# Two-layer transformer block: the second attention is queued by clocks of the engines, which also choose VectorE or GpSimd for each addition of the bias

## The chip, the cores and the metric

The kernel runs on one core of a Trainium2 chip. The metric is the time of one execution on the device in microseconds (us); smaller is better. A core has five engines, each with a queue of its own that it works off in order: TensorE (PE, products; its weight loads are listed as PEld), VectorE (DVE), ScalarE (ACT), GpSimd (POOL) and SyncE (SP), which here only issues transfers (DMA). Engines wait for each other by semaphores.

## The reference

Input `x` is 8 x 512 x 256 in fp32. Layer 0 adds a causal attention (with a latent of 64 for keys and values) and a gated feed-forward of ternary weights to `x`; layer 1 adds an attention with a bias of position and a routed mixture of small experts. What the change orders anew is the attention of layer 1:

```python
qkv = jnp.einsum('bsd,ed->bse', xn, Wqkv)
q, k, v = jnp.split(qkv, 3, axis=-1)            # 16 heads of 16
logits = jnp.einsum('bihd,bjhd->bhij', q, k) * scale + pos_bias[None]
attn = jax.nn.softmax(logits, axis=-1)
out = jnp.einsum('bhij,bjhd->bihd', attn, v).reshape(B, S, D)
x = x + jnp.einsum('bsd,ed->bse', out, Wout) + experts(xn)
```

The bias depends on head and distance alone.

## The kernel before

Four stages follow each other: the first attention, the feed-forward, the second attention, the experts. Between them `x` goes through DRAM (`x1d`, `x2d`, `x3d`; the normalised `x` of layer 1 through `xn1d`, its transposed form through `xt1d`), one image of 512 tokens at a time, in tiles of 128 partitions.

Both attentions are objects of the class `Attention`. An image has 4 jobs of 4 heads each. For one job the queries and keys are loaded from DRAM as high and low fp32r parts, stacked over the partitions (`load`, four transfers on SyncE's queue, with one of four stacks). Then come

- 16 units of `first` (L280): a product `s_ps` of 128 queries with 512 keys for one head, and on VectorE one instruction that adds the bias and takes the smallest value of each row (the signs are turned, so this is the maximum). `ps_s` has three banks.
- `maxima` (L303): the 16 columns of row values are split in two parts, transposed, copied by ScalarE and sent into two more rows of the stack of queries by two transfers, so that the next product subtracts them by itself.
- 16 units of `second` (L324): the product `t_ps` of 128 keys with 512 queries. In the second attention the bias is then added in one of two ways: by VectorE out of PSUM (L348), or by a copy on ScalarE (L350) and an addition on GpSimd in SBUF (L351). `ps_t` has two banks. `exp` (L373) takes the exponential of two heads at once, in place.
- 4 `weigh` (L378): four products of the weights with the values, one per head, summed over the key tiles in one bank `ctx_ps`.
- `take` and `finish`: ScalarE copies the result, TensorE transposes it, VectorE divides by the sums; after the fourth job the output projection is added to `x`.

The order of all instructions is written out by `run` (L455) under a manual schedule: all five queues follow the program's order. A step `n` has four slots. Each slot queues one `first` (six steps ahead, `lag`), one `second`, in slots 0 and 2 an `exp` of the step before, in slot 0 a `weigh` of two steps before, then one piece of the closing work (`close`) and one piece of the work that prepares the next image (`tasks`: `prep_here`, `values1`). `pause` puts two empty pieces between pieces that depend on each other. Which engine adds the bias is fixed:

```python
if r == 0 or (r == 1 and n % 2):
    nc.vector.tensor_tensor(pt[:, r, :], ps, bias, ALU.add)
else:
    nc.scalar.copy(pt[:, r, :], ps)
    nc.gpsimd.tensor_tensor(pt[:, r, :], pt[:, r, :], bias, ALU.add)
```

So of the 64 additions of an image 24 are VectorE's and 40 are GpSimd's. Closing and preparing work of the second attention share the two banks of `ps_m`. `prep_here(b)` normalises, transposes and projects an image and sends queries and keys to DRAM; `values1(b)` makes its values.

In the experts, `go_down` (L1081) makes the products `d_ps`, copies them to `down` (three buffers) and stores them to DRAM (`inter`); for every 16 experts' pairs four gathers bring them back by token group (`back`), and `combine` adds them to `x` and stores `out`. All these transfers are issued on SyncE's queue, where an issue that waits holds up the ones behind it.

Of the kernel before, what the change touches and what calls it, by code (L numbers as in the profile page):

```python
# [21 lines left out]
P = 128  # L22
# [40 lines left out]
def block_kernel(ctx: ExitStack, tc: tile.TileContext, a: dict, out: bass.AP):  # L63
# [15 lines left out]

    x = {}  # L80

    def fetch_x(pool, b, src, tag="x", to=x):
        to[b] = pool.tile([P, TPB, D], F32, tag=tag, name="x")
        nc.sync.dma_start(to[b], src[b * S : (b + 1) * S, :].rearrange("(t p) d -> p t d", p=P))

    def leave_x(b, dst):
        nc.sync.dma_start(dst[b * S : (b + 1) * S, :].rearrange("(t p) d -> p t d", p=P), x[b])

    x1d = dram.tile([B * S, D], F32, name="x1d")
    x2d = dram.tile([B * S, D], F32, name="x2d")  # L90
    x3d = dram.tile([B * S, D], F32, name="x3d")
    xnd = dram.tile([B * P, 2 * S], F32, name="xnd")
    xn1d = dram.tile([B * S, D], F32, name="xn1d")
# [17 lines left out]
    nc.gpsimd.memset(power, -0.5)  # L111
# [5 lines left out]
    def norm_steps(layer, b, pool):  # L117
        for t in range(TPB):
            st = pool.tile([P, 6], F32, tag="bn", name="bn")
            nc.vector.bn_stats(st, x[b][:, t, :])  # L120
            nc.vector.bn_aggr(mv[:, layer, b * TPB + t, :], st)
            if t % 2:
                yield
        ve = pool.tile([P, TPB], F32, tag="ve", name="ve")
        nc.vector.tensor_scalar_add(ve, mv[:, layer, b * TPB : (b + 1) * TPB, 1], EPS)  # L125
        yield
        r0 = pool.tile([P, TPB], F32, tag="r0", name="r0")
        nc.gpsimd.tensor_tensor(r0, ve, power, ALU.pow)  # L128
# [3 lines left out]
        nc.vector.tensor_mul(r2, r0, r0)  # L132
        nc.vector.tensor_mul(r2, r2, ve)
        nc.vector.tensor_scalar(r2, r2, -0.5, 1.5, ALU.mult, ALU.add)
        nc.vector.tensor_mul(rstd[:, layer, b * TPB : (b + 1) * TPB], r0, r2)

    def normalise(layer, b, t, dst, src=None):
        i = b * TPB + t
        nc.vector.tensor_scalar(
# [8 lines left out]
    def transpose_steps(srcs, dst, psum, tag, evacuate):  # L148
        for i in range(0, len(srcs), 2):
            ps = psum.tile([P, 2, 2, P], F32, tag=tag, name="xT_ps")  # L150
            for j in range(2):
                for d in range(2):
                    nc.tensor.transpose(ps[:, d, j, :], srcs[i + j][:, d * P : (d + 1) * P], ident)
# [14 lines left out]
    def split(pool, ps, scale, dst, reverse, bufs):  # L168
# [4 lines left out]
        nc.scalar.activation(hi[:, way], ps, AF.Copy, scale=scale)  # L173
# [3 lines left out]
        nc.vector.scalar_tensor_tensor(lo[:, way], ps, scale, hi[:, way].bitcast(F32), ALU.mult, ALU.subtract)  # L177
# [16 lines left out]

    def pause():

        for _ in range(2):
            yield

    class Attention:  # L200
# [4 lines left out]
        def __init__(self, st, causal, order, lag, stacks, qd, kd, bias_of, w_out, fetch, done, cn_bufs):  # L205
# [10 lines left out]
            self.ps_m = pool("ps_m", 2, space=PSUM)  # L216
# [14 lines left out]
            self.jobs = {}  # L231
            if causal:
                self.mask = self.fixed.tile([P, S], F32, name="mask")
                nc.scalar.dma_start(self.mask, a["cst"][:, C_CAUSAL:])
# [7 lines left out]
        def clear(self, i):  # L242

            qs, ks = self.stacks[i]
            nc.gpsimd.memset(qs[64:, :, :].bitcast(F32), 0.0)
            nc.gpsimd.memset(ks[64:, :, :].bitcast(F32), 0.0)
            nc.gpsimd.memset(ks[ROW_M : ROW_M + 2, :, :].bitcast(F32), -1.0)
            if i < len(self.vst):
                nc.gpsimd.memset(self.vst[i], 1.0)


        def keep_v(self, b, t, v_ps, copy=nc.vector.tensor_copy):

            assert b < len(self.vst) or (b - len(self.vst), 3) in self.taken
# [25 lines left out]
        def first(self, s, r):  # L280
# [6 lines left out]
            nc.tensor.matmul(  # L287
# [11 lines left out]
            nc.vector.tensor_tensor_reduce(  # L299
# [3 lines left out]
        def maxima(self, t):  # L303
# [4 lines left out]
            nc.vector.tensor_copy(by_tile[0], job["least"])  # L308
            nc.vector.tensor_tensor(by_tile[1], job["least"], by_tile[0].bitcast(F32), ALU.subtract)
# [4 lines left out]
            nc.tensor.transpose(ps, parts.rearrange("p l r c -> p (l r c)").bitcast(F32), ident)  # L314
            yield True
            rows = self.work.tile([2 * n, P], F32R, tag="rows", name="rows")
            nc.scalar.copy(rows, ps)
            for part in range(2):
                (nc.scalar if self.causal else nc.sync).dma_start(
                    job["qs"][ROW_M + part : ROW_M + part + 1].bitcast(F32), rows[part * n : (part + 1) * n, :].bitcast(F32)  # L320
                )
            yield

        def second(self, n, r):  # L324
# [3 lines left out]
            lo = j * P if self.causal else 0  # L328
# [9 lines left out]
            nc.tensor.matmul(  # L338
# [6 lines left out]
            if not self.causal:  # L345
                bias = self.bias_of(self.order[t][1], r, j)
                if r == 0 or (r == 1 and n % 2):
# [867 lines left out]
```

## Time and profile before

| | us |
|---|---|
| median of 3 runs | 2205.24 |
| lowest and highest run | 2197.03, 2216.65 |
| the profiled execution | 2195.91 |
| its span, first to last instruction | 2194.2 |

The stages of the profiled execution, by windows of its trace:

| stage | from, to | length | PE busy | DVE busy | ACT busy | POOL busy | DMA share |
|---|---|---|---|---|---|---|---|
| first attention | 0 to 575 | 575 | 479.81 | 380.33 | 241.26 | 121.97 | 0.61 |
| feed-forward | 575 to 1250 | 675 | 660.40 | 323.29 | 155.62 | 8.02 | 0.12 |
| second attention, loads | 1250 to 1296 | 46 | 23.73 | 23.91 | 3.04 | 21.68 | 0.88 |
| second attention | 1296 to 1930 | 634 | 586.75 | 510.14 | 471.16 | 412.93 | 0.46 |
| its end | 1930 to 1945 | 15 | 5.03 | 2.06 | 0.58 | 2.82 | 0.35 |
| experts | 1945 to 2194 | 249 | 174.78 | 98.13 | 67.10 | 42.74 | 0.84 |

In the profile, a group's line gives line of code, engine, operation, output<-inputs, shapes and count, then busy time and the mean of one in ns, then the idle time of the engine just before these instructions and the instructions that ended most of it. A matmul's busy time includes waiting inside the pipeline; the spacing of starts tells what one costs.

### The profile page before, as it was taken

To read this page: it belongs to the slowest core of one execution; us is meant where nothing else is said; L and a number is where in the kernel's file an instruction comes from. 1 tells how busy PE (TensorE), PEld (TensorE's weight loads), DVE (VectorE), ACT (ScalarE), POOL (GpSimd) and SP (SyncE) were. 2 spreads that over 40 slices of the span, in tenths; PEclk is the share of its full clock that TensorE was granted. 3 is DMA by queue.
4 is the path that set the end of the run, shared out by engine and by line. 5 is a ranking of instruction groups with operands and counts; after the bars stand their busy time and mean duration, and the time that the engine had idled before them with its cause. 6 is when DMAs were issued, how large, how long until landed. Compare 5 with 4: busy or idle time off the path is not lost.

```text
span 2194.2 us, 29805 instructions
## 1 busy us (share of the span) xinstructions
PE 1930.5 (88%) x10182; PEld 1259.3 (57%) x10182; DVE 1337.9 (61%) x3621; ACT 938.8 (43%) x1570; POOL 610.1 (28%) x552
## 2 busy tenths in 40 slices
PE   3689999999799999999999779999999999968863
PEld 1345555555488888888888544544544444436652
DVE  3667776677345535535535367888878878735431
ACT  0244444445322212212222137777777778834320
POOL 4211111112100000000000256656656657732200
PEclk8799999999899999999999879999999999989986
DMA  5647767674430000000001384554553554167697
GB/s 126 177 121 175 185 164 195 174 173 109 181 127 30 20 10 29 20 1 20 20 1 49 90 238 98 117 124 91 116 127 89 114 121 77 47 235 204 192 254 204
DMA packets 151905, 254.40 MB, mean 116 GB/s; under 512 B 14382, under 2 KB 84911, under 8 KB 151395
## 3 DMA queue, kind: packets, MB, share of 16 engines
q1 hardware_dynamic: 146418, 245.56, 43.2%
q10 hardware_dynamic: 4864, 6.24, 0.9%
q8 instruction: 82, 1.34, 0.3%
q0 software_dynamic: 464, 0.63, 0.1%
q14 instruction: 77, 0.62, 0.1%
HBM read 171.58 MB, written 91.29 MB: 120 GB/s over the span
## 4 chain that ended last, share of the span: by engine, by line
PE 62%; DMA 12%; DVE 10%; ACT 4%; issue 4%; POOL 1%; SPq 1%; ACTq 1%; POOLq 0%; DVEq 0%
PE hid_ps L780 21%; PE t_ps L338 7%; PE ctx_ps L385 7%; PE s_ps L287 6%; PE proj_ps L522 3%; DMA qs<-rows 3%; DVE junk L299 3%; DMA ks<-kd 3%; PE val L780 3%; PE gate L780 3%; PE ffo L780 2%; PE o_ps L443 2%; DMA back<-inter 1%; DMA inter<-down 1%; PE d_ps L1092 1%
## 5 line engine op out<-in xcount | busy, mean ns | idle before, releaser
L287 PE MATMUL s_ps<-ks,qs 96*128 96x512 f32 (+2 forms) x1024 | 471.0, 468 | 81.6 <-DMA ks<-kd 40.4
L351 POOL TENSOR_TENSOR pt<-pt,bias 128x512 f32<-128x512 f32 x320 | 408.8, 1288 | 242.5 <-ACT pt L350 233.5
L338 PE MATMUL t_ps<-qs,ks 128*128 128x512 f32 (+2 forms) x1024 | 394.8, 391 | 38.1 <-DMA qs<-rows 15.1
L299 DVE CUSTOM_DVE_ANT_0 junk<-s_ps,bias 128x512 f32<-128x512 f32 x512 | 338.0, 686 | 120.3 <-PE s_ps L287 107.2
L287 PEld LDWEIGHTS s_ps<-ks,qs 96*128 96x128 f32 x1024 | 201.9, 198 | 265.6 <-DVE least L299 110.7
L299 DVE CUSTOM_DVE_ANT_0 junk<-s_ps,mask 128x384 f32<-128x384 f32 (+3 forms) x512 | 233.1, 486 | 142.0 <-PE s_ps L287 140.8
L338 PEld LDWEIGHTS t_ps<-qs,ks 128*128 128x128 f32 x1024 | 197.9, 195 | 149.1 <-ACT pt L350 43.2
L376 ACT ACTIVATE pt<-pt 128x1024 f32<-128x1024 f32 x256 | 273.7, 1069 | 3.2 <-POOL pt L351 3.1
L770 DVE CAST h<-hf 128x512 fp32r<-128x512 f32 x192 | 81.2, 426 | 303.2 <-ACT hf L819 302.2
L385 PE MATMUL ctx_ps<-pt,vst 128*32 128x512 f32 (+3 forms) x2048 | 262.5, 533 | 3.7 <-ACT pt L376 2.5
L819 ACT ACTIVATE hf<-hid_ps,sh 128x512 f32<-128x512 f32 x128 | 88.1, 688 | 380.5 <-PE hid_ps L780 374.6
L350 ACT COPY pt<-t_ps 128x512 f32<-128x512 f32 x320 | 184.3, 585 | 151.8 <-PE t_ps L338 150.3
L780 PE MATMUL hid_ps<-h,h1T_m 128*128 128x512 f32 x1024 | 237.4, 391 | 0.0
L780 PE MATMUL hid_ps<-h,h2T_m 128*128 128x512 f32 x1024 | 236.9, 392 | 0.0
L780 PEld LDWEIGHTS hid_ps<-h,h2T_m 128*128 128x128 f32 x1024 | 192.2, 188 | 42.6 <-issue 2.9
L780 PEld LDWEIGHTS hid_ps<-h,h1T_m 128*128 128x128 f32 x1024 | 191.2, 188 | 43.8 <-DVE h L771 2.5
L128 POOL TENSOR_TENSOR r<-ve,power 128x4 f32<-128x4 f32 x16 | 16.2, 1012 | 706.9 <-DVE ve L125 602.9
L363 POOL TENSOR_SCALAR_AFFINE_SELECT pt<-pt 128x512 f32<-128x512 f32 x128 | 81.7, 639 | 404.6 <-ACT pt L353 229.6
L353 ACT ACTIVATE pt<-t_ps 128x512 f32<-128x512 f32 (+1 forms) x256 | 130.3, 546 | 99.9 <-PE t_ps L338 95.0
L348 DVE TENSOR_TENSOR pt<-t_ps,bias 128x512 f32<-128x512 f32 x192 | 131.6, 685 | 15.4 <-PE t_ps L338 14.0
L771 DVE TENSOR_TENSOR h<-hf,h 128x512 fp32r<-128x512 f32 x192 | 132.0, 690 | 5.6
L355 ACT ACTIVATE pt<-t_ps 128x256 f32<-128x256 f32 (+1 forms) x128 | 61.9, 491 | 148.3 <-PE t_ps L338 117.1
(137 smaller groups left out, 2265.2 us busy)
## 6 DMA issues: line engine op xcount, KB each, us to landing
qs<-qd SPq DMA_DIRECT2D x128, 256.0 KB
ks<-kd SPq DMA_DIRECT2D x64, 256.0 KB
ks<-kd SPq DMA_DIRECT2D x128, 128.0 KB
inter<-down SPq DMA_DIRECT2D x32, 512.0 KB
back<-inter SPq DMA_DIRECT2D x32, 512.0 KB
qd<-hi SPq DMA_DIRECT2D x32, 256.0 KB
qd<-lo SPq DMA_DIRECT2D x32, 256.0 KB
kd<-hi SPq DMA_DIRECT2D x32, 256.0 KB
```

Of the source, the lines that this page charges most:

```text
L287: nc.tensor.matmul(ps[:, :n], lhsT=job["qs"][:ROW_M, r, c * P : (c + 1) * P], rhs=job["ks"][:ROW_M, r, :n], start=True, stop=True,)
L299: nc.vector.tensor_tensor_reduce(junk[:, :width], ps[:, :width], add, 1.0, 3e38, ALU.add, ALU.min, job["least"][:, c, r : r + 1])
L338: nc.tensor.matmul(ps[:, base - at : S - at], lhsT=job["ks"][:, r, j * P : (j + 1) * P], rhs=job["qs"][:, r, base:], start=True, stop=True,)
L348: nc.vector.tensor_tensor(pt[:, r, :], ps, bias, ALU.add)
L350: nc.scalar.copy(pt[:, r, :], ps)
L351: nc.gpsimd.tensor_tensor(pt[:, r, :], pt[:, r, :], bias, ALU.add)
L353: nc.scalar.activation(pt[:, r, lo:], ps[:, lo:], AF.Exp, scale=-1.0)
L376: nc.scalar.activation(pt, pt, AF.Exp, scale=-1.0)
L385: nc.tensor.matmul(job["ctx"][32 * r : 32 * r + 32, lo:], lhsT=job["v"][:, j, r, :], rhs=job["p"][j][:, r, lo:], start=(j == 0), stop=(j = ...
L771: nc.vector.tensor_tensor(t[1][:, k, :], value, t[0][:, k, :].bitcast(F32), ALU.subtract)
L780: nc.tensor.matmul(ps, lhsT=l, rhs=r, start=(i == 0), stop=(i == len(pairs) - 1))
L819: nc.scalar.activation(hf, ps, AF.Gelu, scale=scales[sc][:, o : o + 1])
```

## The change

The method `run_by_clock` takes the place of `run` for the second attention. While it writes the program it keeps a clock for each of PE, DVE, ACT and POOL. Every instruction is issued through a small wrapper (`T_`, `V_`, `A_`, `G_`) that moves its engine's clock on by an assumed duration; the instruction itself is the same. 0.6 us are assumed for a hand-over from one engine to another. At each turn the method looks at what could start on TensorE at its present clock (a first product, a second product, a weighing, a piece of closing work, a piece of preparing work), each with the time at which its inputs and its bank would be there, and queues the first that qualifies in a fixed order of preference. If nothing qualifies, TensorE's clock moves on.

```diff
+    HANDOVER = 0.6
+    def takes(engine, op, out, k):
+        if engine == "PE":
+            if op == "transpose":
+                return 0.15
+            n = columns_of(k["rhs"]) * (1 if k["rhs"].dtype == F32R else 4)
+            return 0.013 + n / 2400 * (0.25 if k["lhsT"].shape[-1] == 2 * HD else 1)
+        n = columns_of(out)
+        if engine == "DVE":
+            return 0.08 + n / 960
+        if engine == "ACT":
+            return 0.45 if op == "dma_start" else 0.12 + n / 1140
+        return 0.1 if op == "dma_start" else 0.2 + n / (470 if op == "tensor_tensor" else 4700 / 4)
```

The second products of this attention have their own method, in which the clocks choose the engine of the addition:

```diff
+        def second_biased(self, n, r, at, exps):
...
+            bias = self.bias_of(self.order[t][1], r, j)
+            by_pool = max(clock["POOL"], max(clock["ACT"], at) + 0.5 + HANDOVER) + 1.3
+            if max(clock["DVE"], at) + 0.6 < by_pool - 3.0:
+                V_.after = at
+                V_.tensor_tensor(pt[:, r, :], ps, bias, ALU.add)
+                free = added = clock["DVE"]
+            else:
+                A_.after = at
+                A_.copy(pt[:, r, :], ps)
+                free = clock["ACT"]
+                G_.after = free + HANDOVER
+                G_.tensor_tensor(pt[:, r, :], pt[:, r, :], bias, ALU.add)
+                added = clock["POOL"]
+            self.bank_t = [self.bank_t[1], free + HANDOVER / 2]
+            if r % 2:
+                exps.append((max(added, job["added"]) + HANDOVER, n, r // 2))
+            job["added"] = added
```

The core of the turn (`s` first product, `t` second, `w` weighing, `c` closing, `k` preparing; `u` and `v` count the first and second products queued, `w` the weighings):

```diff
+                while exps and exps[0][0] <= now + HANDOVER:
+                    self.exp(*exps.popleft()[1:], done_at)
...
+                if u < units and u // 16 < loaded and u - v < 40:
+                    s_at = max(bank_s[u % 3], self.stack_at[u // 16])
+                if v < u and v // 16 in self.rows_at and (v % 4 or v // 4 < w + 3):
+                    t_at = max(self.rows_at[v // 16], self.bank_t[0])
+                if w < 4 * jobs and w in done_at and (w % 4 or not takes):
+                    w_at = done_at[w]
...
+                soon = now + 0.05
+                ahead = clock["DVE"] - now
+                if s_at <= soon and ahead < 0.5:
+                    do = "s"
+                elif w_at <= soon and v // 4 - w >= 2:
+                    do = "w"
+                elif c_at <= soon and urgent:
+                    do = "c"
+                elif k_at <= soon and credit >= 1:
+                    do = "k"
+                elif s_at <= soon and ahead < 1.0:
+                    do = "s"
+                elif t_at <= soon and max(clock["ACT"], clock["POOL"] - 1.0) - now < 1.0:
+                    do = "t"
...
```

After these come, without conditions on other clocks, urgent closing work, weighing, closing, preparing, first and second products in that order. The assumed time from the copy of the maxima to their rows in the stack is 3.5 us, from the issue of a load to its stack 8.0 us.

With it go these edits:

```diff
-            self.ps_m = pool("ps_m", 2, space=PSUM)
+            self.ps_m = pool("ps_m", 2 if causal else 1, space=PSUM)
+            self.ps_k = self.ps_m if causal else pool("ps_k", 1, space=PSUM)
...
-        for _ in range(2):
+        for _ in range(2 if slots[0] else 0):
             yield
...
-                att1.tasks.append(iter([None] * 10))
                 att1.tasks.append(values1(0))
...
-            if t % 4 == 0 and t // 4 + 1 < B:
-                att1.tasks.append(prep_here(t // 4 + 1))
-            if t % 4 == 2 and t // 4 + 1 < B:
+            if t == 0:
+                att1.tasks.append(prep_here(1))
+            if t % 4 == 3 and t // 4 + 1 < B:
                 att1.tasks.append(values1(t // 4 + 1))
+            if t % 4 == 3 and t // 4 + 2 < B:
+                att1.tasks.append(prep_here(t // 4 + 2))
```

In the second attention the preparing work (`prep_here`, `values1`) now has a bank of its own, `ps_k`, and the closing work keeps one, `ps_m`; the empty pieces of `pause` are off there. An image is prepared from the last job of the image two before it on.

Two edits lie outside the second attention. `x1d`, `x2d`, `x3d` and `xn1d` change their layout in DRAM, so that what one partition reads or writes of an image is one run of 4 KB instead of four of 1 KB (`combine` reads half of it, a run of 2 KB). And the stores of `down` of the last chunk are issued on ScalarE's queue:

```diff
-    x1d = dram.tile([B * S, D], F32, name="x1d")
+    x1d = dram.tile([B * P, TPB * D], F32, name="x1d")
...
+        return src[b * P : (b + 1) * P, :].rearrange("p (t d) -> p t d", d=D)
...
-                nc.sync.dma_start(half[:, r0 % NH : r0 % NH + NR, :], down)
+                (nc.sync if ch + 1 < B // 2 else nc.scalar).dma_start(half[:, r0 % NH : r0 % NH + NR, :], down)
```

The first attention and the feed-forward keep their order.

## The prediction

> **What bounds the kernel now.** I read the page first (busy shares, then the busy tenths by slice), then the windows by stage, then the groups, waits and timeline inside the second attention, and last SyncE's queue at the end.
>
> ```profile
> PE 1930.5 (88%) x10182; PEld 1259.3 (57%) x10182; DVE 1337.9 (61%) x3621; ACT 938.8 (43%) x1570; POOL 610.1 (28%) x552
> PE   3689999999799999999999779999999999968863
> DVE  3667776677345535535535367888878878735431
> POOL 4211111112100000000000256656656657732200
> ```
>
> Slices 0 to 10 are the first attention, 11 to 22 the feed-forward (TensorE alone, fp32 products back to back), 23 to 35 the second attention, then the experts. The change orders only the second attention anew, so its stage must be read by itself. Two windows from the table by stage, each 80 us:
>
> ```profile
> core 0: us, PE busy (x) PEld busy (x) DVE busy (x) ACT busy (x) POOL busy (x), PEclk, DMA share, GB/s
> 1460.00:1540.00 80.00, 74.22 (x336) 38.76 (x335) 66.16 (x175) 58.20 (x88) 50.56 (x40) 0.96 0.49 107
> 1620.00:1700.00 80.00, 74.20 (x336) 39.10 (x337) 66.28 (x177) 57.81 (x88) 50.17 (x40) 0.96 0.48 110
> ```
>
> The stage repeats: the timeline has the normalisation of the next image at 1590.32, 1672.32 and 1754.09, a period of 81.8 us for one image (64 first products s_ps, 64 second products t_ps, 16 weighings). TensorE seems full at 74 of 80, but a matmul's duration contains waiting. By start-to-start spacing in the timeline (s_ps 1650.30, t_ps 1650.54) a 512-column s or t takes 0.24 us, four weighing products 1.07, two 256-column fp32 products 0.86, four transposes 0.63. One image is 128 x 0.24 + 16 x 1.07 + 16 such fp32 pairs x 0.86 (8 projections, 8 value and 8 output products) + 8 x 0.63 + 4 x 0.28 = 30.7 + 17.1 + 13.8 + 5.0 + 1.1 = 67.7 us. So 14 us of each 81.8 are gaps in TensorE's queue.
>
> ```profile
> L351 POOL TENSOR_TENSOR pt<-pt,bias 128x512 f32<-128x512 f32 x197 | 252.3, 1290 | 149.8 <-ACT pt L350 144.0
> L299 DVE CUSTOM_DVE_ANT_0 junk<-s_ps,bias 128x512 f32<-128x512 f32 x313 | 207.6, 686 | 66.0 <-PE s_ps L287 64.5
> L287 PEld LDWEIGHTS s_ps<-ks,qs 96*128 96x128 f32 x313 | 61.8, 198 | 80.2 <-DVE least L299 30.9 <-DVE pt L348 24.5 <-issue 6.5
> L338 PEld LDWEIGHTS t_ps<-qs,ks 128*128 128x128 f32 x312 | 61.6, 197 | 49.1 <-ACT pt L350 20.9 <-DVE pt L348 11.5 <-issue 4.3
> ```
>
> These are groups of 1380 to 1780 (five images). TensorE waits for a bank that VectorE or ScalarE has yet to empty (80.2 + 49.1 us before its weight loads), while VectorE waits for TensorE (66.0), ScalarE's copy for TensorE (103.6) and GpSimd for ScalarE (149.8). Everybody waits for everybody and nobody is full: the fixed order is the bound, not an engine. Per image VectorE does 64 + 24 instructions at a spacing of 0.61 (1657.23, 1657.84, 1658.45) and some 13.3 of small ones, 67; ScalarE 40 copies at a spacing of 0.48, 32 exponentials at 0.96 and 8 of others, 58; GpSimd 40 x 1.29 = 51.6.
>
> **The change part by part.** *The queueing by clocks and the choice of engine (one answer together).* No arithmetic is added or taken away; the 64 additions of an image are distributed anew. Now 24 are on VectorE (0.61 each) and 40 on ScalarE plus GpSimd (0.48 + 1.29). The new rule takes VectorE only where its finish is over 3 us ahead of GpSimd's, which by its numbers means that GpSimd's clock is 2.3 us later than VectorE's and than the moment the product is there. So GpSimd is preferred until it is all but continuously loaded. If an image takes 75 us and GpSimd is 90% loaded, it gets 0.9 x 75 / 1.29 = 52 additions and VectorE 12. Then GpSimd carries 67, VectorE 67 - 12 x 0.61 = 60, ScalarE 58 + 12 x 0.48 = 64, TensorE 67.7. The load moves from the engine that frees the s banks to one at 63%; TensorE and GpSimd become the highest at about 68. Best end: no gaps, 68. Worst end of this part alone: every addition on GpSimd, 64 x 1.29 = 82.6. Today the fullest engine gets 67.7 of 81.8 (83%); an order that lets an instruction into a queue only when its inputs are due should do better, and the planner's hand-over of 0.6 us is longer than what the timeline shows (GpSimd starts 0.08 us after the copy at 1639.94 ends), so its order has slack in it. I take 90%: 75 us, an estimate. Seven images with that period: 7 x (81.8 - 75) = -48 us (ends -97 and +6).
>
> *The last image* (1860 to 1930, no preparation beside it) has GpSimd at 52 of 70 us. A preference for GpSimd brings it to some 0.95 x 68 / 1.29 = 50 additions, 65 us; the image stays near 68 to 70: 0 (ends -4 and +13, all 64 on GpSimd).
>
> *The start* (1250 to 1296, DMA share 0.88): the padding of ten steps goes, so the value products come behind the first s, where they wait for the tile read back from xt1d (issued on SyncE at 1258.15, used at 1272.47), and some 14 s queue behind them. But t can't start before the first group's maxima, and these now lie behind an s that waits for the second load until 1283.39; the new order puts them ahead of it. The transfers are the same. 0 (ends -5 and +8).
>
> *One bank each for the closing and the preparing work* instead of two shared ones: the planner holds the next piece until the last is emptied on its clocks, and there are 14 us of free TensorE time to hide it; 0 here, and a rival below.
>
> *SyncE and the tail.* In the last chunk eight stores of `down` move from SyncE's queue to ScalarE's.
>
> ```profile
> 2146.00 0.57 SPq L1108 DMA_DIRECT2D back<-inter  x1
> 2149.24 0.69 DVE L75 COPY down<-d_ps 128x512 f32<-128x512 f32 x1 [1.04 <-PE d_ps L1092]
> 2153.40 0.37 SPq L1131 DMA_DIRECT2D out<-x  x1
> 2155.18 9.09 SPq L1102 DMA_DIRECT2D inter<-down  x4
> 2163.15 0.58 ACT L77 COPY down<-d_ps 128x512 f32<-128x512 f32 x1 [12.47 <-DMA inter<-down]
> 2180.91 5.83 PE L1122 MATMUL y_ps<-back,permT 128*32 128x256 f32 x64 [29.17 <-DMA back<-inter]
> ```
>
> This is the timeline of the end, SyncE's issues among it. The stores of the second half were ready from about 2148 (copies at 2146.64 and 2147.51), yet the first is issued at 2155.18, behind gathers and an `out` store that waited for its sum. Then the last copy waits 12.47 us for a free buffer, and the last gather ends at 2180.9. On ScalarE's queue these stores pass that block and start up to 7 us sooner; the transfers compete (DMA share 0.96 from 2100 to 2150), so I take -5 (ends -8 and +1: what queues behind an issue on ScalarE is its next copy of `d_ps`, and an issue has cost 0.4 to 0.5 us there). The eight issues themselves, 4 us of SyncE, go.
>
> *The layouts of x1d, x2d, x3d and xn1d*: runs of 4 KB (2 KB in the combination) instead of 1 KB, no instruction more or less. The store x3d<-x in 1 KB runs moved 330 to 370 GB/s, the f1 load near 400, so some 15% of 7.3 MB in the expert stage, 2 to 3 us of DMA time, partly exposed (the chain has xn<-xn1d with 5.63 and x<-x3d with 4.25). -2 (ends -6 and +1). In the feed-forward (DMA share 0.12 beside 660 of 675 us of TensorE) and both attentions (0.61 and 0.46) they lie beside other work; without that cover each of some 50 transfers of 512 KB would count 0.2 us.
>
> *A rule that speaks against it.* VectorE's reduction lasts 674 to 692 ns over all 481 of the stage, its addition 679 to 693, GpSimd's 1265 to 1352, though they overlap all the time. Two VectorE forms stretch: the normalisation (404 at least, 990 in the middle, up to 1372) and the parts (186 to 1273). The Trainium skill, Perfetto Trace Analysis, section Optimizing Scalar/DVE Operations, warns that GpSimd and VectorE share a port for reading SBUF, so that moving work between the two might not help. If that held for these additions, each of 52 would keep VectorE out for 1.29 us: 67 + 60 = 127 us an image and a much slower kernel. The steady rows (one input in PSUM) say it does not; by the rows only 4 normalisations (0.59 us of stretch each) and 4 parts (0.27) pay, 3.4 us an image, and a third more with GpSimd a third fuller: +1.1 us on VectorE, which then has 15 us to spare. I take the rows.
>
> Sum: -48 + 0 + 0 - 5 - 2 = -55 on the profiled execution's 2195.9 (span 2194.2), 2141. The median of the three runs, 2205.2, is 9.3 above that execution, so 2150.
>
> **The rivals.**
> *GpSimd becomes the bound, and VectorE is hardly ever chosen* (the choice doesn't do what it says). For: the 3 us of preference; while ScalarE's clock limits how fast products are issued, GpSimd's may never fall 2.3 us behind. The planner takes 0.57 and 1.02 us for ScalarE's copy and exponential where the trace spaces them 0.48 and 0.96, so its clocks slow there and give GpSimd the time. Against: bursts of two products push GpSimd's clock ahead quickly. With 0 to 4 additions on VectorE the period is 77 to 82.6: 7 x (-4.8 to +0.8), +9 to +13 for the last image, -7 for tail and layouts: -32 to +12, or 2173 to 2217; about 2200.
>
> *TensorE's queue stalls on the single banks* (slower). The place: 8 preparing and 12 closing fillings of one bank each per image. The price: a filling behind which the bank isn't yet empty holds everything in TensorE's queue; a projection's bank is free only after ScalarE's 0.59 and VectorE's 0.68, and VectorE's clock in the planner knows neither the stretched normalisations nor SyncE's waits. It decides from 14 us an image, 0.7 us for each of the 20. At 0.95 us each the period is 67.7 + 19 = 86.7: +34 - 7 = +27, or 2232. For it: the preparing products have no other bank to go on with. Against: the planner holds the piece back by its clocks plus 0.6 us.
>
> **How the numbers follow.** Forecast 0.63 (2150, by itself 2112 to 2182), GpSimd bound 0.20 (2173 to 2217), single banks 0.17 (2210 to 2260). A difference under 1%, 22 us, can't be told from none. Under 2183 lie nearly all of the forecast and a little of the second case: 0.63. Over 2227: two thirds of the third case and a rest for orders that fit badly in other ways: 0.17. Between: 0.20. The range from 2110 to 2224 leaves out 0.04 below and some 0.13 above.
>
> **What would show it.** Right: images of 72 to 78 us, 48 to 56 additions on GpSimd each, TensorE's waits for banks less than half, the stores of the last chunk on ScalarE's queue before 2150 less what was gained. Wrong: over 60 additions on GpSimd and its busy share at 95% (the second case); waits of the projections', values' or transposes' weight loads for ScalarE or VectorE of some 10 us an image (the third); VectorE's reductions well above 0.69 us (the rule was right).

## The result and the profile after

The changed kernel takes 2225.4 us (median of 11 runs, 2218.2 to 2232.1), the kernel before beside it 2199.2 us (11 runs, 2191.3 to 2216.7): a ratio of 1.0108, 95% interval 1.0083 to 1.0134. It is 1.1% slower, and just above the range that was given. The profiled span is 2221.1 us against 2194.2, so 26.9 us are to be found.

First the page of the changed kernel, its totals and some rows of busy tenths:

```profile
PE 1923.9 (87%) x10182; PEld 1248.7 (56%) x10182; DVE 1319.0 (59%) x3530; ACT 985.6 (44%) x1661; POOL 717.9 (32%) x643
PE   3799998999799999999999688889898888869873
POOL 4211111111100000000000356677787887952200
```

GpSimd has 91 instructions more than before, ScalarE 91 more, VectorE 91 fewer: the choice moved 91 of 512 additions from VectorE to GpSimd. In the second attention (slices 23 to 35, counted from 0) TensorE mostly shows 8 where it had 9.

To see where the time went, I took the last context copy of each image (`cx<-ctx_ps` on ScalarE, the end of its attention but for the closing work) as a mark. Those of images 1, 2 and 6 in the timeline of the kernel before, then of the same images after; the columns are start, length, engine, line, operation:

```profile
1380.57 0.58 ACT L397 COPY cx<-ctx_ps 128x512 f32<-128x512 f32 x1
1462.03 0.59 ACT L397 COPY cx<-ctx_ps 128x512 f32<-128x512 f32 x1
...
1789.57 0.58 ACT L397 COPY cx<-ctx_ps 128x512 f32<-128x512 f32 x1
```

```profile
1402.12 0.60 ACT L123 COPY cx<-ctx_ps 128x512 f32<-128x512 f32 x1
1495.00 0.60 ACT L123 COPY cx<-ctx_ps 128x512 f32<-128x512 f32 x1
...
1823.16 0.59 ACT L123 COPY cx<-ctx_ps 128x512 f32<-128x512 f32 x1
```

(Line 123 is the wrapper through which all instructions of this attention are now issued.) The first image ends 21.6 us later, 2 to 3 of which are a later start of the stage. The second takes 92.9 us instead of 81.5, +11.4. From there on little happens: images 3 to 6 take 82.0 us on average after and 81.9 before; images 3 to 7 together lose 3.3 us, and the eighth gains 1.7. The way from the last copy to the experts adds 1.0, and the experts' stage itself gains 8.7 (240.7 us after 249.4). Together 21.6 + 11.4 + 3.3 - 1.7 + 1.0 - 8.7 = 26.9 us. So two things have to be explained: why the steady part did not gain, and what the first two images lost.

The steady part in windows of 80 us, the second of which lies where one of the prediction's did:

```profile
core 0: us, PE busy (x) PEld busy (x) DVE busy (x) ACT busy (x) POOL busy (x), PEclk, DMA share, GB/s
1460.00:1540.00 80.00, 70.07 (x323) 36.75 (x323) 61.80 (x158) 59.96 (x95) 59.78 (x48) 0.96 0.44 103
1620.00:1700.00 80.00, 71.39 (x329) 36.60 (x329) 63.50 (x162) 63.86 (x99) 64.25 (x52) 0.98 0.45 105
```

GpSimd does 52 additions and is busy for 64 of 80 us; VectorE fell from 66 to 63, ScalarE rose from 58 to 64. Load moved from VectorE to the other two, as intended; no engine is full, and still no image is shorter. The groups of 1380 to 1780 show what is new:

```profile
L123 POOL TENSOR_TENSOR pt<-pt,bias 128x512 f32<-128x512 f32 x241 | 303.5, 1285 | 97.6 <-ACT pt L123 95.2 <-DMA ks<-kd 1.0
L123 DVE CUSTOM_DVE_ANT_0 junk<-s_ps,bias 128x512 f32<-128x512 f32 x298 | 197.5, 685 | 90.3 <-PE s_ps L123 89.5
...
L123 DVE TENSOR_TENSOR parts<-least,parts 128x16 fp32r<-128x16 f32 x19 | 17.0, 897 | 0.7
L123 DVE CAST parts<-least 128x16 fp32r<-128x16 f32 x19 | 13.4, 704 | 0.0
L123 PE MATMUL m_ps<-ident,parts 128*32 128x128 f32 x19 | 5.4, 284 | 22.0 <-DVE parts L123 22.0
```

The same two small instructions before the change:

```profile
L309 DVE TENSOR_TENSOR parts<-least,parts 128x16 fp32r<-128x16 f32 x20 | 9.2, 459 | 0.7
L308 DVE CAST parts<-least 128x16 fp32r<-128x16 f32 x20 | 3.5, 174 | 0.0
```

VectorE's reductions and GpSimd's additions last what they lasted. But the two small instructions that split the maxima went from 0.17 and 0.46 us to 0.70 and 0.90, and TensorE's transpose of them, which had waited for nothing, now waits. One such place in the timeline from 1502 to 1505.3 (lines of other tiles left out), and the longest cast of all, from 1870 to 1874:

```profile
1502.47 3.74 POOL L123 TENSOR_TENSOR pt<-pt,bias 128x512 f32<-128x512 f32 x3 [2.56 <-ACT pt L123]
1502.66 1.14 DVE L123 CAST parts<-least 128x16 fp32r<-128x16 f32 x1
1503.83 1.19 DVE L123 TENSOR_TENSOR parts<-least,parts 128x16 fp32r<-128x16 f32 x1
1505.14 0.09 PEld L123 LDWEIGHTS m_ps<-ident,parts 128*32 128x32 f32 x1 [2.02 <-issue]
1505.17 0.27 PE L123 MATMUL m_ps<-ident,parts 128*32 128x128 f32 x1 [1.74 <-DVE parts L123]
...
1869.93 3.74 POOL L123 TENSOR_TENSOR pt<-pt,bias 128x512 f32<-128x512 f32 x3
1870.37 3.34 DVE L123 CAST parts<-least 128x16 fp32r<-128x16 f32 x1
```

GpSimd's three additions end near 1503.8, 1505.0 and 1506.2; the cast ends with the first, the subtraction with the second. This holds throughout: of the 32 casts in the changed kernel 29 begin while GpSimd is adding, and all 29 end 36 to 42 ns after the end of an addition; of the 32 subtractions 22 begin so and all end 43 to 48 ns after one. The 3 and 10 others last 0.17 to 0.19 us. Before, 2 casts and 7 subtractions began during an addition and 30 and 25 did not. So, as the ends show it, the two instructions, whose operands all lie in SBUF, wait for GpSimd's addition to end; the reductions and VectorE's own additions, which read PSUM, last 683 to 688 ns on average whether they begin during an addition or not.

The waits over the whole attention (1290 to 1960; total, times, longest):

```profile
PE m_ps L123 <- DVE parts L123: 38.8, 26, 3.3
PEld m_ps L123 <- issue: 34.0, 17, 3.7
...
PE s_ps L123 <- DMA ks<-kd: 17.6, 13, 3.7
```

The waits of PE and PEld must not be added: at 1505 the weight load's 2.02 us and the product's 1.74 us are one and the same stop. (The expectation of `e3_late` below adds them, to 83 us, and that of `e11_h15corr` to 61 us.) By the products, TensorE stands still for 38.8 us ahead of the transposes of the maxima (none before), and for 17.6 us ahead of first products whose load hasn't landed (3.1 before). TensorE's queue is in order, so all behind it stands too. One such load in the timeline:

```profile
1396.07 0.97 SPq L337 DMA_DIRECT2D qs<-qd  x2
1398.39 0.31 SPq L340 DMA_DIRECT2D ks<-kd  x1
1407.99 0.76 PE L123 MATMUL s_ps<-ks,qs 96*128 96x512 f32 x1 [3.74 <-DMA ks<-kd]
1408.80 0.69 DVE L123 CUSTOM_DVE_ANT_0 junk<-s_ps,bias 128x512 f32<-128x512 f32 x1 [4.06 <-PE s_ps L123]
```

The planner allowed 8.0 us from the issue; here it was 12, and TensorE and VectorE stood. These two waits were my first theory of the loss. The experiments show how much of it they are.

Last the end of the changed kernel:

```profile
2165.04 0.33 ACTq L1337 DMA_DIRECT2D inter<-down  x1
2169.36 0.59 ACT L77 COPY down<-d_ps 128x512 f32<-128x512 f32 x1 [2.57 <-DMA inter<-down]
```

The stores now go out on ScalarE's queue, and the longest wait of a copy for a free buffer is 2.57 us instead of 12.47.

### The profile page after: what moved, and what is told of

It reads as the page before. It is cut to its first block, busy times and chain, and to the rows that moved or that the text cites. A ratio compares the mean times of both kernels' runs of the same rounds, so it can differ in the third digit from the quotient of the medians.

```text
span 2221.1 us, 29855 instructions
## 1 busy us (share of the span) xinstructions
PE 1923.9 (87%) x10182; PEld 1248.7 (56%) x10182; DVE 1319.0 (59%) x3530; ACT 985.6 (44%) x1661; POOL 717.9 (32%) x643
## 4 chain that ended last, share of the span: by engine, by line
PE 62%; DMA 13%; DVE 10%; issue 5%; ACT 4%; SPq 2%; POOL 1%; ACTq 1%; POOLq 0%; DVEq 0%
PE hid_ps L1012 21%; PE ctx_ps L123 6%; PE t_ps L123 6%; PE s_ps L123 6%; DMA ks<-kd 5%; DMA qs<-rows 4%; PE proj_ps L123 3%; DVE junk L123 3%; PE val L1012 3%; PE gate L1012 3%; PE o_ps L123 2%; DVE parts L123 2%; PE ffo L1012 2%; ACT pt L123 2%; PE v_ps L123 2%
## 5 line engine op out<-in xcount | busy, mean ns | idle before, releaser
L123 POOL TENSOR_TENSOR pt<-pt,bias 128x512 f32<-128x512 f32 x411 | 516.8, 1285 | 165.8 <-ACT pt L123 136.1
L123 PE MATMUL s_ps<-ks,qs 96*128 96x512 f32 (+2 forms) x1024 | 428.4, 428 | 76.5 <-DMA ks<-kd 50.3
L123 PE MATMUL t_ps<-qs,ks 128*128 128x512 f32 (+2 forms) x1024 | 424.2, 421 | 35.6 <-DMA qs<-rows 20.1
L123 ACT ACTIVATE pt<-t_ps 128x512 f32<-128x512 f32 (+2 forms) x384 | 192.9, 528 | 252.2 <-PE t_ps L123 216.8
L123 ACT COPY pt<-t_ps 128x512 f32<-128x512 f32 x411 | 233.1, 595 | 131.4 <-PE t_ps L123 123.6
L1002 DVE CAST h<-hf 128x512 fp32r<-128x512 f32 x192 | 81.1, 425 | 303.3 <-ACT hf L1051 302.3
L123 PE MATMUL ctx_ps<-pt,vst 128*32 128x512 f32 (+3 forms) x2048 | 253.4, 549 | 2.5 <-ACT pt L123 1.4
L123 POOL TENSOR_SCALAR_AFFINE_SELECT pt<-pt 128x512 f32<-128x512 f32 x128 | 81.6, 637 | 410.3 <-ACT pt L123 410.2
L1037 ACT ACTIVATE sg<-gate,s 128x512 f32<-128x512 f32 x64 | 44.2, 690 | 112.1 <-PE gate L1012 109.7
L123 PEld LDWEIGHTS ctx_ps<-pt,vst 128*32 128x32 f32 x2048 | 45.0, 110 | 83.4 <-issue 55.5
```

What stands on the lines that cost most here:

```text
L123: return f(*args, **k)
L1002: nc.vector.tensor_copy(t[0][:, k, :], value)
L1037: nc.scalar.activation(sg, gate, AF.Silu, scale=scales["s1"][:, o : o + 1])
```

## The experiments

Each is measured against the kernel before, run beside it. "Images 3 to 6" is the mean period between the marks described above; "planned" is the same period as the planner's own clock has it while it writes the program, without any chip. A period comes from one profiled execution. How far it can be trusted is seen from two pairs of runs that queue the pieces of their middle images in the very same order (`e9_start` and the changed kernel, `e12_h3thr1start` and `e4_h3thr1`): they agree within 0.4 us.

**The parts outside the attention.** `e1_plus` is the kernel before with the layouts and ScalarE's queue for the last stores, and nothing else.

```diff
-    x1d = dram.tile([B * S, D], F32, name="x1d")
+    x1d = dram.tile([B * P, TPB * D], F32, name="x1d")
...
-                nc.sync.dma_start(half[:, r0 % NH : r0 % NH + NR, :], down)
+                (nc.sync if ch + 1 < B // 2 else nc.scalar).dma_start(half[:, r0 % NH : r0 % NH + NR, :], down)
```

> The kernel before with the two edits outside the second attention alone: the layouts of x1d, x2d, x3d, xn1d and the last chunk's stores on ScalarE's queue. The expert stage of the changed kernel is 4 us shorter than before, so every theory expects -4 us (ratio 0.998, between 0.995 and 1.000). If these two edits are what costs time, the ratio is over 1.003.

Measured: 0.9954 (0.9941 to 0.9967), -10 us; its images take 81.6 us. So if the parts add up, the order of the attention alone costs 1.0108 / 0.9954 = 1.0155, about 34 us. The two edits were not separated. Of the 13.0 us between the two profiled spans, 5.4 lie ahead of the first image's mark (1375.19 against 1380.57) and 5.8 behind the last one.

**Fixed split under the new clocks.** `e2_fixed` keeps the queueing and gives VectorE its old 24 additions of an image.

```diff
-            if max(clock["DVE"], at) + 0.6 < by_pool - 3.0:
+            if r == 0 or (r == 1 and n % 2):
```

> The changed kernel with the fixed split of the additions back (24 on VectorE, 40 on GpSimd per image), the order still by clocks. Theory 'choice' (GpSimd too full: it holds the small VectorE instructions up and makes the last image 14 us longer): the parts of the maxima last below 0.3 us on average again instead of 0.7 to 0.9, and the time falls by 25 to 40 us to about 2190. Theory 'plan' (the order by clocks is slow in itself; the planner's own clock shows a period of 80.7 us with the fixed split and 80.8 with the choice): the period of an image stays at 81 to 83 us and the time within 12 us of the changed kernel.

Measured: 1.0159 (1.0112 to 1.0205), images 3 to 6 at 87.3 us against 82.0 with the choice. The intervals of the times overlap, but the periods lie far apart. So the choice isn't what costs; it is the queueing. The parts stay stretched here too (means of 0.50 and 0.96 us from 1380 to 1780), though GpSimd has its old 40 additions: 27 casts and 20 subtractions begin during one. It is the moment at which they are queued that changed, not how full GpSimd is.

**The two waits.** `e3_late` lets the planner queue the transpose of the maxima 3 us later, `e10_stk` lets it use a load 12 us after its issue instead of 8, `f1_stklate` does both.

```diff
-                        self.stack_at[loaded] = now + 8.0
+                        self.stack_at[loaded] = now + 12.0
...
                     ready_at[kind] = max([clock[e] for e in touched], default=clock["PE"]) + HANDOVER
+                    if kind == "close":
+                        ready_at[kind] += self.parts_late
+                        self.parts_late = 0.0
```

Here `maxima` sets `parts_late` to 3.0.

> The changed kernel, but the transpose of the maxima is queued 3 us later on the planner's clock, so that TensorE's queue no longer stands before VectorE's parts (83 us of waiting before m_ps in the changed kernel). Theory 'stall' (this waiting is the loss): the wait before m_ps falls under 20 us and the time by 30 us or more, to about 2190. Theory 'plan': the wait before m_ps falls, other waits take its place, and the time changes by less than 10 us.

> The changed kernel, with 12 us assumed from the issue of a load to its stack in place of 8 (in the trace a load issued at 1396.1 was waited for at 1408.0, and TensorE stood 3.7 us before it). Theory 'wrong times' (the planner's too short times make the queues stand): TensorE's waits for ks<-kd fall from 22 to under 8 us and the time falls by 10 to 20 us. Theory 'own pace' (the plan's period of 81 us is the bound of the steady part and a wait removed comes back elsewhere): the waits fall, the images from the third on stay at 80 to 83 us and the time within 6 us.

> The changed kernel with both times corrected at once: 12 us for a load, the transpose of the maxima 3 us later; hand-over 0.6 and preference of 3 us as they are. The planner's own clock gives 83.3 us per image. Theory 'stalls' (TensorE's queue standing before loads and before the maxima takes back what the order by clocks would give): with both gone the images from the third on come at 75 to 78 us and the time is 2175 or less. Theory 'own pace' (the order that these constants write is itself no faster than before): 79.5 to 83 us per image, and 2185 to 2205, the gain against the changed kernel lying in the first two images.

Measured: `e3_late` 1.0095 (1.0059 to 1.0131), images 3 to 6 at 81.1; `e10_stk` 1.0026 (1.0009 to 1.0043), 82.1; `f1_stklate` 1.0059 (1.0038 to 1.0079), 79.9. The waits of `f1_stklate` over the whole attention, and a window of 80 us with the columns as above:

```profile
PE s_ps L123 <- DMA ks<-kd: 9.6, 7, 2.6
...
PEld m_ps L123 <- issue: 1.7, 1, 1.7
```

```profile
1650.00:1730.00 80.00, 76.05 (x346) 38.31 (x345) 64.59 (x169) 67.31 (x107) 69.37 (x56) 0.98 0.49 116
```

Of TensorE's 38.8 us at the maxima next to nothing is left, of the 17.6 us at the loads 9.6, and an image still takes 80: TensorE's idle time has turned into busy time (76 of 80, against 70 and 71), which contains waiting. In images 3 to 6 the two waits were 18.9 + 5.2 us in the changed kernel and are 4.0 here: 5 us an image were taken away, and an image became 2 shorter. All waits of TensorE's products in these four images come to 22.6 us before the change, 33.6 after it and 20.0 here. The theory that the two waits keep the steady part at 82 us falls. What `e10_stk` gains (it is the faster of the three) lies in the first two images: they end at 1394.92 and 1474.76 instead of 1402.12 and 1495.00. In `f1_stklate`, with the same 12 us, they end at 1404.71 and 1493.54, so this gain belongs to that one order and not to the load's time as such.

**The start.** `e9_start` holds the preparing work back for 25 us, in case it pushes the first image; `g1_lead24` cuts the lead of the first products over the second from 40 to 24 units.

```diff
-            ready_at["tasks"] = 0.0
+            ready_at["tasks"] = 25.0
```

```diff
-                if u < units and u // 16 < loaded and u - v < 40:
+                if u < units and u // 16 < loaded and u - v < 24:
```

> The changed kernel, but no preparing work is queued in the first 25 us of the planner's clock. Theory 'start': in the changed kernel the first image ends 21.5 us later than before (copy of its last context at 1402.1 against 1380.6), because the value products stand in TensorE's queue for a tile still in flight and the store of the normalised image stands in SyncE's queue ahead of the bias tiles. It expects this copy at 1385 to 1392 and 10 to 17 us less in all, about 2210. If the start is bound by the volume of its loads instead, the copy stays at 1398 or later and the time within 5 us.

> The changed kernel with first products at most 24 units ahead of the second ones instead of 40, as far as in the kernel before (six steps of four). Theory 'lead' (the first image ends 21.5 us later because TensorE and VectorE first build up a lead of 16 more units, which the last images don't pay back since GpSimd and ScalarE set their pace): the copy of the first image's last context comes at 1385 to 1392 instead of 1402, the last images lose less than 5 us, and the time falls by 8 to 15 us. Theory 'loads' (the first two images are late because of loads planned too short): 1398 or later, and the time within 5 us.

In `e9_start` part of the first image's weighings is queued ahead of the values that they use, so these terms differ from the reference's. Measured: 1.0091 (1.0060 to 1.0123), the first image ends at 1404.35: no gain in the first image, so the preparing work in those 25 us is not its cause. `g1_lead24`: 0.9981 (0.9966 to 0.9996), its marks and waits:

```profile
1380.31 0.60 ACT L123 COPY cx<-ctx_ps 128x512 f32<-128x512 f32 x1
1464.02 0.60 ACT L123 COPY cx<-ctx_ps 128x512 f32<-128x512 f32 x1
```

```profile
PEld m_ps L123 <- issue: 35.4, 16, 4.1
PE m_ps L123 <- DVE parts L123: 32.2, 23, 3.7
```

The first two images end 31 us earlier than with a lead of 40 and where they ended before the change. The eighth takes 71.3 us instead of 63.0: 8 of the 31 us came back there, as they would if the long lead had done its first products in advance. The wait for loads is down to 1.1 us. The waits at the maxima are mostly still there (32.2 us by the products), and images 3 to 6 take 81.9, once more. The first image ends at 1389 to 1412 in all 15 orders with a lead of 40 in this document, and at 1380 and 1384 in the two with 24 and 28.

**The constants of the choice.** The hand-over that the planner assumes (0.6 us) and the preference for GpSimd (3.0 us) were varied. `e4_h3thr1`:

```diff
-    HANDOVER = 0.6
+    HANDOVER = 0.3
...
-            if max(clock["DVE"], at) + 0.6 < by_pool - 3.0:
+            if max(clock["DVE"], at) + 0.6 < by_pool - 1.0:
```

> The changed kernel with two constants of the planner changed: 0.3 us for a hand-over in place of 0.6, and VectorE is chosen when it is 1 us ahead in place of 3. The planner's own clock shows a period of 71.8 us in place of 80.8. Theory 'plan': the chip follows with some loss, a period of 74 to 78 us and a time of 2160 to 2190. Theory 'stall': hand-overs are given less time, so TensorE's queue stands longer before what is late, above all before m_ps, and the time is 2210 or more.

> The changed kernel with 0.3 us for a hand-over in place of 0.6, the choice of engine as it is (VectorE from 3 us ahead). The planner's own clock gives a period of 77 us in place of 80.8. If the assumed hand-over is the larger part of what e4_h3thr1 gained (61 us on the changed kernel): a period of 77 to 79 and a time of 2180 to 2195. If the threshold is the larger part: 2205 to 2220.

> The changed kernel with VectorE chosen from 1 us ahead in place of 3, hand-over 0.6 as it is. The planner's own clock gives 77.4 to 82.7 us per image. If the threshold is the larger part of the gain of e4_h3thr1: 30 or more additions of an image on VectorE and a time of 2175 to 2195. If the hand-over is: 2200 to 2220. In both the last image loses its 13 us against before.

> The order by clocks with a hand-over of 0.3 us and the fixed split of the additions. The planner's own clock gives 74.1 us per image. If the order alone carries the gain and the choice is worth little: within 10 us of e4_h3thr1, 2160 to 2180. If a free choice is needed (with the fixed split an order by clocks was slower than with the choice: ratio 1.016 against 1.011): 2190 or more.

> Hand-over 0.15 us, VectorE from 2 us ahead. The planner's own clock gives 69.4 to 71 us per image, the shortest of all tried. If the chip follows the plan with 3 to 4 us of loss: a period of 73 to 75 and 2140 to 2160. If hand-overs assumed this short are not met any more (TensorE's queue stands before late inputs): the period is over 77 and the time over 2170, with more waiting before weight loads than in e4_h3thr1.

| run | edit | ratio (95%) | images 3 to 6, us | planned, us |
|---|---|---|---|---|
| after | 0.6, 3.0 | 1.0108 (1.0083 to 1.0134) | 82.0 | 80.8 |
| `e4_h3thr1` | 0.3, 1.0 | 0.9859 (0.9828 to 0.9890) | 75.9 | 71.8 |
| `e5_h3` | 0.3, 3.0 | 1.0025 (1.0012 to 1.0038) | 80.3 | 77 |
| `e6_thr1` | 0.6, 1.0 | 1.0091 (1.0060 to 1.0121) | 81.5 | 79 |
| `e7_h3fixed` | 0.3, fixed 24 | 1.0143 (1.0100 to 1.0187) | 85.9 | 74.1 |
| `e8_h15thr2` | 0.15, 2.0 | 1.0105 (1.0074 to 1.0135) | 83.7 | 70 |

`e4_h3thr1` beats both kernels: 2164.6 us against 2197.4 (4 runs of it). One of its windows:

```profile
1490.00:1570.00 80.00, 74.46 (x359) 40.26 (x356) 74.50 (x196) 60.99 (x86) 43.24 (x34) 1.00 0.53 124
```

From the second to the seventh image it has 32 additions on VectorE and 32 on GpSimd (34 and 30 on the mean of all eight), far from the 12 and 52 of the forecast, with VectorE at 93% and GpSimd at little over half. Either constant alone doesn't do it. `e6_thr1` puts 46 additions of an image on VectorE on average, which makes VectorE the bound by the spacings of the prediction: (64 + 46) x 0.61 + 13 = 80 us.

**What makes that version fast?** I tried its split without its clocks, its clocks with a fixed split, and its clocks with one other constant corrected.

> The kernel before, its order by slots untouched, with 32 instead of 24 additions of an image on VectorE (heads 0 and 1). The fastest kernel so far (hand-over 0.3, VectorE from 1 us ahead) has 34 there. Theory 'order' (what makes it fast is the order by clocks): this kernel is within 1% of before or slower, since VectorE, already at 67 of 81.8 us, gets 5 us more in a fixed order. Theory 'split' (fewer additions on the long way over ScalarE and GpSimd are enough): images of 76 to 79 us, 2155 to 2180.

> Order by clocks with a hand-over of 0.3 us, but a fixed split with 32 additions of an image on VectorE (heads 0 and 1), close to the 34 that the free choice takes with 1 us. If the number on VectorE is what matters, 75 to 78 us per image and 2160 to 2180. If the moment of each choice matters (with a fixed split of 24 the same order gave 85 us): 82 us or more and 2200 or more.

> The fastest so far (e4_h3thr1: hand-over 0.3, VectorE from 1 us ahead, images of 75 to 77 us) with the start of e9_start. If the start is what theory 'start' says, its first image, at 1389.3 there, ends at 1375 to 1382 and the time is 8 to 12 us shorter than e4_h3thr1's 2164.6; if not, within 4 us of it.

> The fastest so far (hand-over 0.3, VectorE from 1 us ahead; 2164.6) with 12 us assumed for a load. Its waits for ks<-kd are only 10 us in all, and VectorE is busy for some 73 of its 75.7 us per image. Theory 'VectorE is the bound there': within 8 us of it, 2157 to 2172. Theory 'stalls': 10 to 15 us less, 2150 to 2155.

> The fastest so far (hand-over 0.3, VectorE from 1 us ahead, 2164.6) with the lead at most 28 instead of 40. The planner's own clock gives 72.2 us per image, as for the fastest (71.8). If the chip follows such a plan: 75 to 77 us per image and 2150 to 2165. If the fastest is a lucky order (with only the load's assumed time changed, planned 74, it fell back to 81 us): 79 to 84 us and 2185 or more.

> As e8_h15thr2 (hand-over 0.15, VectorE from 2 us ahead: planned 70 us an image, measured 84), with the two times that were too short corrected: 12 us for a load, and the transpose of the maxima 1.5 us later. The planner's own clock gives 73 us. Theory 'wrong times': the waits before m_ps (61 us) and for loads go, and the images come at 75 to 77 us, about 2160. Theory 'too tight' (a hand-over of 0.15 leaves no slack for anything that the clocks don't know): 80 us or more an image and 2200 or more.

| run | edit | ratio (95%) | images 3 to 6, us | planned, us |
|---|---|---|---|---|
| `f2_split32` | before's order by slots, VectorE takes `r < 2` (32) | 1.0024 (1.0014 to 1.0035) | 82.8 | none |
| `f4b_h3clock32` | hand-over 0.3, fixed 32 | 1.0128 (1.0093 to 1.0164) | 82.1 | 76.2 |
| `e12_h3thr1start` | `e4_h3thr1`, preparing work 25 us later | 0.9918 (0.9892 to 0.9943) | 76.5 | 72.1 |
| `f3_h3thr1stk` | `e4_h3thr1`, load 12 us | 1.0039 (1.0027 to 1.0050) | 81.3 | 74 |
| `g2_h3thr1lead28` | `e4_h3thr1`, lead 28 | 0.9979 (0.9961 to 0.9997) | 80.9 | 72.2 |
| `e11_h15corr` | `e8_h15thr2`, load 12 us, maxima 1.5 us later | 0.9987 (0.9964 to 1.0010) | 79.7 | 73.1 |

`e12_h3thr1start` has the early weighings of `e9_start` too. From its fourth image on it queues TensorE's pieces in the same order as `e4_h3thr1` and gives each addition to the same engine; images 4 to 6 take 76.2 us there and 75.9 here. So the 76 us repeat where the order repeats, but this pair is one order run twice and no second order that is fast. A load time nearer to the truth, or a shorter lead, writes another order and brings it back to 81, at much the same split (`f3_h3thr1stk` gives VectorE 35 additions of an image on average). A fixed 32, the very number of the fast order's middle images, doesn't get there in either order. So the number on VectorE isn't the reason, nor the hand-over alone, and what the fast order has that its neighbours lack stays open. Over all 17 orders written by the clocks, planned and measured period have a correlation of 0.27: planned 70 to 83, measured 76 to 87.

## Why the prediction was wrong

**The steady part, -48, was the step that failed.** "An order that lets an instruction into a queue only when its inputs are due should do better", 90% of the fullest engine, 75 us: measured +0.2 us an image in images 3 to 6, and +13.0 over images 2 to 8, nearly all of it in the second. Of the 14 us of gaps an image that I worked out from spacings, 22.6 / 4 = 5.7 show as waits of TensorE's products in the trace before; that this order would close them was inferred from what the planner meant to do, and they grew to 33.6 / 4 = 8.4. Two things spoke against it. Its own clock, which can be read off without a chip and which I did not work out, with the constants of the change, needs 80.8 us an image, so followed exactly the plan had 1 us to give; in none of the runs did the measured period fall more than 3.4 us below the planned one (`f1_stklate`: 79.9 against 83.3), so 75 would have been far outside all that was seen. And I took the 0.6 us for a hand-over that the trace shows at 0.08 us for slack to be recovered; the plan spends it instead. Halving it shortened the image (with the smaller preference to 75.9 us, alone to 80.3), but it also writes another order, and a quarter of it (with a preference of 2.0) gave 83.7; no simple rule turns the planned period into the measured one. So the failed step is known, and the cause of the steady period, order by order, is not.

**The start, 0 with ends of -5 and +8, failed too**, by +21.6 us in the first image and +11.4 in the second. I looked at the value products, which the padding had held back, and not at `u - v < 40`, which stood in the diff. With 24 in its place the 31 us are gone, and for the first image all 17 orders point the same way (1389 or later with 40, 1384 or earlier with less). For the second image it is not the only cause: with 40 in place, `e5_h3` ends it at 1470.39 and `e10_stk` at 1474.76. Of the parts of the loss, waits for loads that the trace names make up 10.7 us of the first two images in the changed kernel (1.1 with 24), and 8 came back in the eighth image; the rest was not told apart. The clock granted to TensorE is lower there as well (0.90 from 1296 to 1380, 0.97 before, 0.96 with a lead of 24), but so is TensorE's work, and which of these follows the other was not told apart.

**The last image, 0:** -1.7 came, but by luck: with a lead of 24 it takes 71.3 us, 6.6 more than before, and the long lead took 8.3 off that.

**Split and loads of the engines:** 52 additions on GpSimd and 12 on VectorE were forecast, and images 2 to 6 have exactly that. Two errors cancel in it, though: GpSimd is 80% busy in an image of 82 us, not 90% in one of 75. The rival of GpSimd as the bound fell with it: GpSimd has 16 of 80 us free.

**Tail and layouts, -5 and -2:** right in sign, and -10 us for the two (interval -13 to -7), so a little more than forecast; the wait for a buffer went from 12.47 to 2.57 us. Their profile places some 5 us of the gain ahead of the first image, where the layouts were forecast to bring nothing.

**Single banks (the slower rival):** its sign came true, its place did not. The projections' weight loads waited 11.4 us for VectorE in the whole attention; the rival needed 14 us an image to begin to count. What stalls TensorE in order is the transpose of the maxima and the loads, and taking both stalls away won 2 us an image. The separate bank, the dropped pauses and the earlier preparing work were not undone one by one, so what each of them costs is not known.

**The shared port.** The rows were the right guide for the instructions that read PSUM: reductions stay at 685 ns beside a GpSimd that is a third fuller. For the small ones my +1.1 us an image was too low: the two instructions of the parts alone went up by (0.70 - 0.17) + (0.90 - 0.46) = 0.97 us, four times an image, 3.9 us. I scaled their stretch with GpSimd's load, but it goes by the moment: 9 of the 64 fell into an addition before, 51 after. They are short, but TensorE waits for them; in `e3_late`, where the transposes no longer wait for them, an image is 1 us shorter.

The chances: 0.17 was given to slower (over 2227), and the time lies 1.4 us above the range. The error was to take one mechanism's best case for 63% while nothing in the profile said that this plan would reach it.

## What to carry to other kernels

When a hand-written order is replaced by a planner's, work out the planner's own clock first: a plan that promises itself 80.8 us an image is no ground for a forecast of 75. Its times have to come from the trace, the landing of loads and the small instructions that stretch included, but better times did not by themselves make better orders here, so measure several orders rather than rank them by their plan, and before two runs are taken to confirm each other, see whether they are the same order. Idle time ahead of a named wait is worth what its removal brings in a run (here 2 of 5 us an image), and the stops of a weight load and of its product, being the same time, are counted once. A lead of one product over its partner was paid for at the start here, and only partly returned at the end.

## What was not expected of the hardware

A cast of 128 x 16 elements on VectorE, 174 ns on average before, took up to 3343 ns, while the 128 x 512 reductions with one input in PSUM kept their 685 ns in the same stretch: what an instruction loses beside GpSimd does not go by its size. In all 20 traces every cast and every subtraction of the parts that begins outside GpSimd's additions of the bias lasts 0.17 to 0.19 us; in the changed kernel each of the 51 that begin inside one ends 36 to 48 ns after the end of an addition. This need not be the addition in hand: the cast of 3343 ns began in the first of three that follow without a gap and ended with the third. The normalisation, with all operands in SBUF too, went from 975 to 1121 ns on average. And the four transfers of a stack took about 12 us from the first issue to the use with the DMA engines 0.36 busy (1380 to 1420).
